# A selective-scan kernel: the input of every fourth state made by ScalarE and TensorE instead of GpSimd

## The chip, the cores and the metric

The kernel runs on one core of one Trainium2 chip (trn2). The core has five engines that work side by side, each through its own instructions in order: TensorE (PE, matrix products and transposes), VectorE (DVE), ScalarE (ACT), GpSimd (POOL) and SyncE (SP, which here only issues the transfers). The metric is the device time in microseconds (us) from launch to end, the median of several runs.

## The reference

Sixteen sequences `x[b]` of 256 steps by 256 features go through four layers that are conditioned on a vector per sequence: a low-rank adapter, a two-way selective state-space layer with an MLP, an attention layer with 16 heads of 64, and an attention layer with 16 heads of 16. Nearly all the time goes into the second one. For each sequence and each of two directions (the backward one runs on the flipped sequence) it computes, with 512 channels d and 64 states s:

```python
xz = h @ in_w;  xs, z = split(xz);  xs = silu(xs)
proj = xs @ xproj_w
dt = softplus(proj[:, :512] + dt_bias);  Bm, Cm = proj[:, 512:576], proj[:, 576:]
A = -exp(A_log)
# for every time t:
hst = hst * exp(dt_t[:, None] * A) + (dt_t * x_t)[:, None] * B_t[None, :]
y_t = einsum('ds,s->d', hst, C_t)
# then
out = ((y + xs * Dskip) * silu(z)) @ out_w
```

For one state s that is: a decay `exp(dt * A[:, s])` for all channels and times, an input `dt * x * B[:, s]`, a scan along time, a multiply by `C[:, s]`, and a sum over the 64 states.

## The kernel before

**Layout.** A channel lies on a partition and time runs along the free dimension, so one state of one sequence and direction is a tile `h` of 128 partitions by 4 channel chunks by 256 times (128x1024 f32). There are 32 units (sequence, direction) and 64 states in each: 2048 steps `k`, taken one after another in the main loop (L1145).

**A step** takes these parts:
- `drive(k + 4)`, L913: four steps ahead. Each four states `load_b` has the DMA spread four rows of B over all partitions (tile `bb`, 512 KB); each eight states `load_c` does so for three rows of C (tile `cb`, 384 KB). Then POOL multiplies `dtx` by a row of `bb` into a fresh `h` (L931). At state 0 ACT also makes `skip = xs * D` (L926).
- `scan(k)`, L965: DVE scans `h` in place in two halves of 512 elements (L974), with the decays as the other operand. For the backward direction it reads `h` from the end. Then `h` is multiplied by C. For states with s % 8 in (0, 2, 3, 5, 6) DVE does it (L977), and C comes from the PSUM tile `cs`; for the other three of each eight POOL does it (L981), from `cb`.
- `decay(k + 1)`, L935: ACT writes the four decays of the next state (L946, one for each chunk, the scale being a column of A) into two of three PSUM banks `decays`, which go round by halves of a state. Column 0 of each chunk holds a zero written once, which starts the scan afresh in each chunk, so a decay covers 255 elements.
- `add_up(k - 2)`, L984: TensorE transposes `h` and adds it to the PSUM tile `y` (eight 128x128 transposes, L992). After that the buffer of `h` is free; there are NH = 11 of them.
- `spread`, L955: TensorE spreads a column of the transposed C (`cT`) into `cs` by two transposes (L961), two such states ahead.

PSUM's eight banks are: three `decays`, one `cs`, two for `y`, two that all other work shares (`bank1`, `bank2`).

**Beside the steps** run generators, of which each step advances two: `pend` (the end of the unit before: `back`, L465, then the projections of the unit after: `front`, L373) and `other` (`rest`, L729: MLP and both attention layers of a finished sequence). `front` makes `xz` (L398, L399), `bc` and its copy in DRAM `bd`, `cT`, `dt` and `dtx` (the last by POOL, L452 to L461). The order in which each engine gets its instructions is a planner's: the order of the program sets priorities, and only calls marked `keep_in_program_order` are held to it. The transfers all go through SP's queue in order. After the last unit, the rest of the last sequence runs alone, and takes the PSUM banks of the scan as well (`alone`, L1183).

Of the kernel before, what the change touches and what calls it, by code (L numbers as in the profile page):

```python
# [23 lines left out]
EPS = 1e-5  # L24

# [29 lines left out]
def kernel(ctx: ExitStack, tc: tile.TileContext, a: dict, out: bass.AP):  # L55
# [69 lines left out]
    ND = 3  # L125
    NH = 11
# [8 lines left out]
    ps_c = ctx.enter_context(tc.tile_pool(name="ps_c", bufs=1, space=PSUM))  # L135
# [120 lines left out]
    for d in ("fwd", "bwd"):  # L256
# [3 lines left out]
        nc.vector.tensor_scalar(an, an, -1.0, None, ALU.mult)  # L260
# [6 lines left out]

    decays = [ps_y.tile([P, 2, T], F32, name=f"decay{j}") for j in range(ND)]
    for dc in decays:
        nc.vector.memset(dc[:, :, 0:1], 0.0)  # L270
# [102 lines left out]
    def front(u):  # L373
# [14 lines left out]
        xz = s2.tile([P, 2 * IC, T], F32, name="xz")  # L388
        for m in range(0, 2 * IC, 2):
            px = halves(bank1("pxz"))  # L390
            for j in range(2):
                for c in range(DC):
                    nc.tensor.matmul(  # L393
                        px[:, j], w_in[:, c, (m + j) * P : (m + j + 1) * P], hT[:, c],
                        start=(c == 0), stop=(c == DC - 1),
                    )
                yield
            nc.scalar.copy(xz[:, m : m + 2], px)  # L398
        nc.scalar.activation(xz, xz, AF.Silu)  # L399
# [3 lines left out]
        for c in range(IC):  # L403
            nc.tensor.matmul(pb[:, :T], w_bc[d][:, c], xz[:, c], start=(c == 0), stop=(c == IC - 1))
# [5 lines left out]
        pt = bank1("pct")  # L410
        for t in range(NT):
            nc.tensor.transpose(pt[:, t * P : (t + 1) * P], bc[:, t * P : (t + 1) * P], ident)
        cT = s2.tile([P, NT, NS], F32, name="cT")
        nc.scalar.copy(cT, pt[:, :T].rearrange("p (t s) -> p t s", t=NT)[:, :, NS:])
        yield


        pr = s1.tile([P, IC, T], F32, name="pr")
        for m in range(0, IC, 2):
            pp = halves(bank1("pdt"))  # L420
            for j in range(2):
                for c in range(IC):
                    nc.tensor.matmul(  # L423
                        pp[:, j], w_dt[:, c, (m + j) * P : (m + j + 1) * P], xz[:, c],
# [36 lines left out]
        tc.keep_in_program_order(nc.gpsimd.tensor_tensor(dtx, dt, xz[:, 0:IC], ALU.mult))  # L461
        st[u] = (xz, cT, bd, dt, dtx)
        yield

    def back(u, yg):  # L465
# [12 lines left out]
        for m in range(DC):  # L478
            xb = xs[b][:, m]
            nc.vector.scalar_tensor_tensor(  # L480
                xb, po[:, m], m_mamba[:, 4 + m, b : b + 1], xb, ALU.mult, ALU.add
# [82 lines left out]
    def heads2(q, k, v, o, rows):  # L564

        exs, exTs = {}, {}
        for i in range(16 + 3):
# [30 lines left out]
            if i % 2 and i >= 3:  # L598
                yield
                po = bank2("po")[:, :T]  # L600
                for h in (i - 3, i - 2):
                    exT = exTs.pop(h)
                    base = (h % 2) * 64
                    for kt in range(NT):
                        nc.tensor.matmul(  # L605
                            po[base : base + 64], v[:, kt, h * 64 : (h + 1) * 64], exT[:, kt],
# [57 lines left out]
    def heads3(q, k, v, oT):  # L664
# [28 lines left out]
        def values(g):  # L693
# [15 lines left out]
            for j in range(4):  # L709
                for kt in range(NT):  # L710
# [182 lines left out]
    bbs, cbs, ys, made, hs, skips = {}, {}, {}, {}, {}, {}  # L893
    cs = ps_c.tile([P, 2, T], F32, name="cs")
    steps = [(u, s) for u in range(len(units)) for s in range(NS)]
    turn = [0]

    def load_b(u, g):
        bd = st[u][2]
        bb = s3.tile([P, SG, T], F32, name="bb")  # L900
        nc.sync.dma_start(bb, bd[g * SG : (g + 1) * SG, :].partition_broadcast(P))
        bbs[u, g] = bb

    def load_c(u, g):
        bd = st[u][2]
        cb = s3.tile([P, 3, T], F32, name="cb")
        nc.sync.dma_start(
            cb,
            bd[NS + 8 * g + 1 : NS + 8 * g + 8 : 3, :].partition_broadcast(P),
        )  # L910
        cbs[u, g] = cb

    def drive(k):  # L913
        u, s = steps[k]
        if s % SG == 0:
# [4 lines left out]
            if s % 8 == 0:  # L920
                load_c(u, s // 8)
        if s == 0:
# [5 lines left out]
        h = s3.tile([P, IC, T], F32, name="h", bufs=NH)  # L928
        bb = bbs[u, s // SG][:, s % SG]
        tc.keep_in_program_order(  # L930
            nc.gpsimd.tensor_tensor(h, st[u][4], bb.unsqueeze(1).to_broadcast([P, IC, T]), ALU.mult)  # L931
        )
        hs[k] = h

    def decay(k):  # L935
        u, s = steps[k]
        d = units[u][1]

        when = slice(1, T) if d == 0 else slice(T - 2, None, -1)
        made[k] = []  # L940
        for i in range(2):
            dc = decays[turn[0] % ND]
            turn[0] += 1
            for j in range(2):
                c = 2 * i + (j if d == 0 else 1 - j)
                nc.scalar.activation(  # L946
                    dc[:, j, 1:T], st[u][3][:, c, when], AF.Exp, scale=a_neg[d][:, c, s : s + 1]
                )
            made[k].append(dc)


    near = [k for k, (u, s) in enumerate(steps) if s % 8 in (0, 2, 3, 5, 6)]
    nth = {k: i for i, k in enumerate(near)}

    def spread(i):  # L955

        if i >= len(near):
            return
        u, s = steps[near[i]]
        for t in range(NT):  # L960
            nc.tensor.transpose(  # L961
                cs[:, i % 2, t * P : (t + 1) * P], st[u][1][:, t, s : s + 1].to_broadcast([P, P]), ident
            )

    def scan(k):  # L965
        u, s = steps[k]
        d = units[u][1]
        h = hs[k]
        for i, dc in enumerate(made.pop(k)):
            hv = h[:, 2 * i : 2 * i + 2].rearrange("p c t -> p (c t)")  # L970
            dv = dc.rearrange("p c t -> p (c t)")
            if d == 1:
                hv = hv[:, ::-1]
            nc.vector.tensor_tensor_scan(hv, dv, hv, 0.0, ALU.mult, ALU.add)  # L974
        if k in nth:
            c = cs[:, nth[k] % 2]
            nc.vector.tensor_tensor(h, h, c.unsqueeze(1).to_broadcast([P, IC, T]), ALU.mult)  # L977
        else:
            c = cbs[u, s // 8][:, (s % 8) // 3]
            tc.keep_in_program_order(  # L980
# [234 lines left out]
```

## Time and profile before

| | |
|---|---|
| median of 3 runs | 7621.71 us (7621.5 to 7629.53) |
| span of the profiled execution | 7616.3 us |
| DVE busy | 6860.6 us (90%) |
| POOL busy | 6843.8 us (90%) |
| PE busy, weight loads | 6249.2 us (82%), 4952.4 us (65%) |
| ACT busy | 5431.2 us (71%) |
| DMA | 675.90 MB, mean 89 GB/s |
| first 400 us / last 226 us: DVE busy | 257.64 / 57.63 us |

The time of the profiled execution itself is not listed apart; its span, from the first instruction to the last, lies 5 us under the median of the runs. A row of the profile's groups reads: line, engine, operation, output<-inputs, shapes, count | busy us, mean ns of one | idle time just before, and who ended it. Instructions of one engine overlap a little, so busy time divided by count is the cost in a sequence, and is a little less than the mean. A matmul's end is modelled, so PE's busy share is not its share of peak.

### The profile page before, as it was taken

How to read it: one execution, taken by the hardware profiler on the slowest of the kernel's cores; microseconds unless marked ns; L12 is line 12 of the kernel's file. 1: busy time of each engine (PE TensorE's matmuls, PEld its weight loads, DVE VectorE, ACT ScalarE, POOL GpSimd, SP SyncE). 2: the span in 40 equal slices, each digit the busy share in tenths (PEclk: the TensorE clock that was granted, in tenths of full speed). 3: DMA queues.
4: the chain of work that ended last, by engine and by line, in shares of the span. 5: the costliest groups of instructions: out<-in, count | busy, mean ns of one | idle time of the engine just before them, and what ended most of it. 6: DMA issues, size and time to landing. Idle time of an engine off the chain costs nothing.

```text
span 7616.3 us, 100847 instructions
## 1 busy us (share of the span) xinstructions
PE 6249.2 (82%) x35471; PEld 4952.4 (65%) x35471; DVE 6860.6 (90%) x6887; ACT 5431.2 (71%) x12141; POOL 6843.8 (90%) x2959
## 2 busy tenths in 40 slices
PE   7568888888888888888888888888888888888778
PEld 4456676666667666676666666666666766666655
DVE  3988999999999999999999999999999999999982
ACT  4567777777777777777777777777777777777753
POOL 3999999999999999999999999999999999999960
PEclk8679999999999999999999999999999999999999
DMA  4112232222322222232222223222232222322221
GB/s 166 54 65 92 89 102 76 87 92 88 103 85 93 80 91 95 92 103 73 88 92 91 100 86 98 78 92 93 87 106 79 94 84 89 101 91 89 73 68 49
DMA packets 331644, 675.90 MB, mean 89 GB/s; under 512 B 24724, under 2 KB 204032, under 8 KB 326784
## 3 DMA queue, kind: packets, MB, share of 16 engines
q1 hardware_dynamic: 331136, 669.44, 26.7%
q8 instruction: 280, 4.59, 0.2%
q14 instruction: 228, 1.87, 0.1%
HBM read 650.22 MB, written 10.75 MB: 87 GB/s over the span
## 4 chain that ended last, share of the span: by engine, by line
DVE 47%; POOL 15%; issue 14%; ACT 12%; PE 10%; DVEq 0%; POOLq 0%; ACTq 0%
DVE h L974 34%; POOL h L931 8%; DVE h L977 8%; ACT decay L946 5%; POOL h L981 5%; PE y L992 3%; DVE maxima L682 1%; ACT L155 1%; PE dense L500 1%; PE down L511 1%; PE bank L108 1%; PE po L605 1%; POOL uu L452 1%; POOL dt L458 1%; POOL dtx L461 1%
## 5 line engine op out<-in xcount | busy, mean ns | idle before, releaser
L974 DVE TENSOR_TENSOR_SCAN h<-decay,h 128x512 f32<-128x512 f32 x4096 | 4748.8, 1213 | 283.1 <-ACT decay L946 196.6
L931 POOL TENSOR_TENSOR h<-dtx,bb 128x1024 f32<-128x1024 f32 x2048 | 4793.5, 2367 | 129.2 <-PE y L992 128.4
L992 PE MATMUL y<-ident,h 128*128 128x128 f32 x16384 | 2385.3, 292 | 693.0 <-POOL h L981 639.1
L992 PEld LDWEIGHTS y<-ident,h 128*128 128x128 f32 x16384 | 2054.6, 151 | 1047.6 <-POOL h L981 733.1
L946 ACT ACTIVATE decay<-dt,a_neg_bwd 128x255 f32<-128x255 f32 x4096 | 1816.8, 471 | 759.9 <-DVE h L974 718.3
L946 ACT ACTIVATE decay<-dt,a_neg_fwd 128x255 f32<-128x255 f32 x4096 | 1824.6, 474 | 613.0 <-DVE h L974 571.6
L981 POOL TENSOR_TENSOR h<-h,cb 128x1024 f32<-128x1024 f32 x768 | 1813.2, 2361 | 289.8 <-DVE h L974 275.1
L977 DVE TENSOR_TENSOR h<-h,cs 128x1024 f32<-128x1024 f32 x1280 | 1533.5, 1215 | 66.2 <-PE cs L961 56.6
L961 PE MATMUL cs<-ident,cT 128*128 128x128 f32 x2560 | 521.6, 294 | 131.8 <-DVE h L977 130.3
L961 PEld LDWEIGHTS cs<-ident,cT 128*128 128x128 f32 x2560 | 331.4, 147 | 216.0 <-DVE h L977 192.0
L572 PE MATMUL sc<-k,q 64*128 64x256 f32 x960 | 293.4, 429 | 16.7 <-ACT ex L581 16.0
L393 PE MATMUL pxz<-hTm,w_in 128*128 128x256 f32 x1024 | 267.6, 388 | 15.9 <-DVE maxima L682 12.1
L679 PE MATMUL sc<-kd,qk 128*128 128x512 f32 x490 | 251.4, 614 | 33.5 <-DVE maxima L682 20.8
L700 PE MATMUL scT<-qk,kd 128*128 128x256 f32 x984 | 251.1, 386 | 28.7 <-DVE qk L691 23.2
L581 ACT ACTIVATE ex<-sc,nmax 128x256 f32<-128x256 f32 x480 | 222.7, 468 | 71.2 <-DVE nmax L577 68.5
L423 PE MATMUL pdt<-xz,w_dt 128*128 128x256 f32 x1024 | 247.3, 385 | 0.0
L572 PEld LDWEIGHTS sc<-k,q 64*128 64x128 f32 x960 | 172.6, 200 | 105.3 <-issue 34.2
L393 PEld LDWEIGHTS pxz<-hTm,w_in 128*128 128x128 f32 x1024 | 181.4, 194 | 53.1 <-DVE maxima L682 15.5
L700 PEld LDWEIGHTS scT<-qk,kd 128*128 128x128 f32 x984 | 175.5, 190 | 60.7 <-ACT pr L429 25.0
L577 DVE TENSOR_REDUCE nmax<-sc 128x2 f32<-128x512 f32 x240 | 163.9, 683 | 49.5 <-PE sc L572 48.8
L423 PEld LDWEIGHTS pdt<-xz,w_dt 128*128 128x128 f32 x1024 | 190.7, 194 | 22.2
L595 ACT COPY exT<-pt 128x512 f32<-128x512 f32 x240 | 140.0, 583 | 86.2 <-PE pt L591 84.0
(350 smaller groups left out, 7571.4 us busy)
## 6 DMA issues: line engine op xcount, KB each, us to landing
bb<-bd SPq DMA_DIRECT2D x512, 512.0 KB
cb<-bd SPq DMA_DIRECT2D x256, 384.0 KB
l2w<-in_L_cond_W_dram SPq DMA_DIRECT2D x32, 1024.0 KB
l3w<-in_L_cond_W_dram SPq DMA_DIRECT2D x32, 1024.0 KB
l1w<-in_L_cond_mlp_w_dram SPq DMA_DIRECT2D x48, 512.0 KB
w_in<-in_L_cond_fwd_in_w_dram SPq DMA_DIRECT2D x16, 1024.0 KB
w_dt<-_L_cond_fwd_xproj_w_dram SPq DMA_DIRECT2D x16, 1024.0 KB
w_in<-in_L_cond_bwd_in_w_dram SPq DMA_DIRECT2D x16, 1024.0 KB
```

The lines of the kernel that those rows point to most:

```text
L393: nc.tensor.matmul(px[:, j], w_in[:, c, (m + j) * P : (m + j + 1) * P], hT[:, c], start=(c == 0), stop=(c == DC - 1),)
L423: nc.tensor.matmul(pp[:, j], w_dt[:, c, (m + j) * P : (m + j + 1) * P], xz[:, c], start=(c == 0), stop=(c == IC - 1),)
L572: nc.tensor.matmul(sc[:, t], q[base : base + 64, ch, t * P : (t + 1) * P], k[base : base + 64, ch], start=True, stop=True,)
L679: nc.tensor.matmul(sc, q[:, g, t * P : (t + 1) * P], kd[g % 2][:, 2 * i : 2 * i + 2], start=True, stop=True)
L700: nc.tensor.matmul(sc[:, kt], kd[g % 2][:, j, kt * P : (kt + 1) * P], q[:, g], start=True, stop=True)
L931: nc.gpsimd.tensor_tensor(h, st[u][4], bb.unsqueeze(1).to_broadcast([P, IC, T]), ALU.mult)
L946: nc.scalar.activation(dc[:, j, 1:T], st[u][3][:, c, when], AF.Exp, scale=a_neg[d][:, c, s : s + 1])
L961: nc.tensor.transpose(cs[:, i % 2, t * P : (t + 1) * P], st[u][1][:, t, s : s + 1].to_broadcast([P, P]), ident)
L974: nc.vector.tensor_tensor_scan(hv, dv, hv, 0.0, ALU.mult, ALU.add)
L977: nc.vector.tensor_tensor(h, h, c.unsqueeze(1).to_broadcast([P, IC, T]), ALU.mult)
L981: nc.gpsimd.tensor_tensor(h, h, c.unsqueeze(1).to_broadcast([P, IC, T]), ALU.mult)
L992: nc.tensor.matmul(ys[u][:, t, c * P : (c + 1) * P], h[:, c, t * P : (t + 1) * P], ident, start=(s == 0 and n == 0 and c == 0), stop=(s == ...
```

## The change

Work moves between engines for every fourth state (s % 4 == 3):
- Its input is no longer made by POOL. Once per unit `turn` has TensorE transpose `dtx` (8 transposes) and ACT copy it to `xT`, time on partitions (2 copies of 128x512). For each fourth state `scale` has ACT multiply `xT` by the column of B (`bT`, per partition) in two activations of 128x512, and `put_in` has TensorE transpose the result (8 transposes) into PSUM. Its decays go to SBUF, into the `h` tile, and the scan takes decays from SBUF and inputs from PSUM.
- The four PSUM banks of the scan (three `decays` and `cs` before) become two `slots` of two banks, one for even and one for odd states, written and scanned by halves. A state's decays, or the fourth state's inputs, go there. The scan of an even state writes its result to its slot in PSUM; that of an odd state to `h`.
- The multiply by C, whole for 1024 elements, is DVE's for even states (from the slot to `h`) and POOL's for odd ones. C comes by DMA for all states: `cb` has four rows each four states (512 KB), `bb` three (384 KB). `spread` and `cs` go.
- For the backward direction `xz` is turned when it is copied from PSUM, and the result of `back` is read turned, so scans and decays run forward. Decays cover 256 elements; `dt` gets 1e34 in column 0 (POOL, once per unit), whose decay is zero, and A is held below -1e-30.
- `xz` becomes `xv` (one buffer) and `zv`, and Silu runs on each. NH falls from 11 to 10. In two attention products beside the scan the matmuls are put in another order (heads inside, key halves outside).

```diff
-        nc.vector.tensor_scalar(an, an, -1.0, None, ALU.mult)
+        nc.vector.tensor_scalar(an, an, -1.0, LEAST, ALU.mult, ALU.min)
...
-    decays = [ps_y.tile([P, 2, T], F32, name=f"decay{j}") for j in range(ND)]
+    slots = [ps_y.tile([P, IC, T], F32, name=f"slot{j}") for j in range(2)]
...
-            nc.scalar.copy(xz[:, m : m + 2], px)
-        nc.scalar.activation(xz, xz, AF.Silu)
+            to = (xv, zv)[m // IC][:, m % IC : m % IC + 2]
+            nc.scalar.copy(to, px[:, :, ::-1] if d else px)
+        for v in (xv, zv):
+            nc.scalar.activation(v, v, AF.Silu)
...
+        tc.keep_in_program_order(nc.gpsimd.memset(dt[:, :, 0:1], APART))
...
-                for h in (i - 3, i - 2):
-                    exT = exTs.pop(h)
-                    base = (h % 2) * 64
-                    for kt in range(NT):
+                for kt in range(NT):
+                    for h in (i - 3, i - 2):
+                        base = (h % 2) * 64
...
-        bb = s3.tile([P, SG, T], F32, name="bb")
+        bb = s3.tile([P, SG - 1, T], F32, name="bb")
...
+    def turn(u):
+        xT = s1.tile([P, NT, DI], F32, name="xT")
+        for t in range(NT):
+            pt = bank1("pxt")
+            for c in range(IC):
+                nc.tensor.transpose(pt[:, c * P : (c + 1) * P], st[u][4][:, c, t * P : (t + 1) * P], ident)
+            nc.scalar.copy(xT[:, t], pt)
+        xTs[u] = xT
...
-        cb = s3.tile([P, 3, T], F32, name="cb")
+        cb = s3.tile([P, SG, T], F32, name="cb")
+        nc.sync.dma_start(cb, bd[NS + g * SG : NS + (g + 1) * SG, :].partition_broadcast(P))
...
-        h = s3.tile([P, IC, T], F32, name="h", bufs=NH)
-        bb = bbs[u, s // SG][:, s % SG]
+        if s % SG < SG - 1:
+            h = s3.tile([P, IC, T], F32, name="h", bufs=NH)
+            bb = bbs[u, s // SG][:, s % SG]
...
+        if s % SG < SG - 1:
+            dcs = two(s)
+        else:
+            h = hs[k] = s3.tile([P, IC, T], F32, name="h", bufs=NH)
+            dcs = h[:, 0:2], h[:, 2:4]
+        for c in range(IC):
+            nc.scalar.activation(
+                dcs[c // 2][:, c % 2], st[u][3][:, c], AF.Exp, scale=a_neg[d][:, c, s : s + 1]
+            )
+
+    def scale(k):
+        u, s = steps[k]
+        sx = s1.tile([P, NT, DI], F32, name="sx")
+        for t in range(NT):
+            nc.scalar.mul(sx[:, t], xTs[u][:, t], st[u][5][:, t, s : s + 1])
+        scaled[k] = sx
+
+    def put_in(k):
+        sx = scaled.pop(k)
+        for c in range(IC):
+            for t in range(NT):
+                nc.tensor.transpose(
+                    two(steps[k][1])[c // 2][:, c % 2, t * P : (t + 1) * P], sx[:, t, c * P : (c + 1) * P], ident
                 )
...
+        c = cbs[u, s // SG][:, s % SG].unsqueeze(1).to_broadcast([P, IC, T])
+        for i, ps in enumerate(two(s)):
+            hv = h[:, 2 * i : 2 * i + 2]
+            d0, d1 = (hv, ps) if s % SG == SG - 1 else (ps, hv)
+            to = hv if s % 2 else ps
+            nc.vector.tensor_tensor_scan(flat(to), flat(d0), flat(d1), 0.0, ALU.mult, ALU.add)
+        if s % 2 == 0:
+            nc.vector.tensor_tensor(h, slots[0], c, ALU.mult)
         else:
+            tc.keep_in_program_order(nc.gpsimd.tensor_tensor(h, h, c, ALU.mult))
...
             scan(k)
             if k + 1 < len(steps):
-                decay(k + 1)
+                if s % SG == SG - 2:
+                    put_in(k + 1)
+                else:
+                    decay(k + 1)
+                if s % SG == SG - 3:
+                    scale(k + 2)
+                    decay(k + 2)
+            if s == NS - 2 and k + 2 < len(steps):
+                turn(u + 1)
```

## The prediction

> **What bounds the kernel now.** I read the busy line of the page first, then the costliest groups, then one steady stretch cut out by time, then the waits inside that stretch.
>
> ```profile
> PE 6249.2 (82%) x35471; PEld 4952.4 (65%) x35471; DVE 6860.6 (90%) x6887; ACT 5431.2 (71%) x12141; POOL 6843.8 (90%) x2959
> ...
> DVE 47%; POOL 15%; issue 14%; ACT 12%; PE 10%; DVEq 0%; POOLq 0%; ACTq 0%
> ```
>
> DVE and POOL are level at 90%, and the chain that ends last runs mostly on DVE. The groups say on what:
>
> ```profile
> L974 DVE TENSOR_TENSOR_SCAN h<-decay,h 128x512 f32<-128x512 f32 x4096 | 4748.8, 1213 | 283.1 <-ACT decay L946 196.6
> L931 POOL TENSOR_TENSOR h<-dtx,bb 128x1024 f32<-128x1024 f32 x2048 | 4793.5, 2367 | 129.2 <-PE y L992 128.4
> ...
> L946 ACT ACTIVATE decay<-dt,a_neg_bwd 128x255 f32<-128x255 f32 x4096 | 1816.8, 471 | 759.9 <-DVE h L974 718.3
> L946 ACT ACTIVATE decay<-dt,a_neg_fwd 128x255 f32<-128x255 f32 x4096 | 1824.6, 474 | 613.0 <-DVE h L974 571.6
> L981 POOL TENSOR_TENSOR h<-h,cb 128x1024 f32<-128x1024 f32 x768 | 1813.2, 2361 | 289.8 <-DVE h L974 275.1
> L977 DVE TENSOR_TENSOR h<-h,cs 128x1024 f32<-128x1024 f32 x1280 | 1533.5, 1215 | 66.2 <-PE cs L961 56.6
> ```
>
> Busy time over count gives what one costs in sequence: a scan 1.159 us, a multiply by C 1.198 on DVE and 2.361 on POOL, an input multiply 2.341 on POOL, a decay 0.4445 on ACT. ACT's long idle time ahead of the decays is ACT waiting for DVE to free a bank: ACT has room.
>
> The steady stretch runs from one unit's four-scan piece in the chain to the same piece 18 units later, so it holds 288 rounds of four states:
>
> ```profile
> 3060.25:7142.51 4082.26, 3423.34 (x19785) 2719.70 (x19784) 3830.89 (x3836) 3038.78 (x6822) 3848.47 (x1657) 0.95 0.28 90
> ```
>
> The columns are length, then PE, PEld, DVE, ACT and POOL busy. Over 288, **a round takes 14.17 us, with DVE busy 13.30, POOL 13.36, PE 11.89, ACT 10.55**. The waits inside that stretch (total, times, longest):
>
> ```profile
> ACT decay L946 <- DVE h L974: 679.6, 781, 4.6
> ...
> DVE h L974 <- ACT decay L946: 113.7, 116, 3.2
> ...
> ACT q L609 <- PE po L605: 82.2, 36, 4.9
> POOL h L931 <- PE y L992: 79.8, 54, 5.8
> ...
> DVE h L974 <- POOL h L931: 41.0, 27, 2.5
> ```
>
> With DVE's smaller waits in the same answer (23.9 for cs; for branch work 25.7 at nmax, 22.9 for the layer norm's bank, 16.4 for a dense product) DVE waits per round 0.395 us for decays, 0.14 for POOL's inputs, 0.08 for cs and 0.23 for branch work: 13.30 + 0.85 + 0.03 unlisted = 14.17. So DVE sets the rate, POOL right beside it.
>
> **The change, per round of four states (512 rounds in the run).**
>
> *DVE.* Multiplies by C fall from 2.5 to 2 a round: 256 fewer x 1.198 = 307 us, or 0.60 a round, so 12.70. The 4096 scans stay. For even states the scan now writes PSUM and the multiply reads PSUM and the cb tile. No row has a scan that writes PSUM. The nearest pair is L804 against L1173, the same 128x512 multiply with its PSUM operand in the one place and the other, at 670 and 689 ns; 19 ns on 2048 scans is 39 us either way (0.08 a round). I take nothing and keep the 0.08 in the range: the scan already reads PSUM, and at 1.16 us for 512 elements it is paced by its recurrence.
>
> *POOL.* It loses 512 input multiplies (x 2.341 = 1198) and gains 256 multiplies by C (x 2.361 = 604): -594 us, 1.16 a round, so 12.20. One small memset a unit is nothing. DVE's wait on POOL (0.14) should shrink; I take half.
>
> *TensorE.* 4096 + 256 transposes come, 2560 (cs) go. At y's price (2385.3 / 16384 = 0.146 us) for the new ones that is 635 - 522 = +113 us, at cs's own price (0.204) +366: 0.2 to 0.7 a round, so at most 12.6. PE stays under DVE. The put_in transposes stand ahead of add_up on PE and need the scan two states back and the scaled input. That scan is over by then, and add_up's y is only needed when a buffer comes round, so I add nothing. DVE's wait for cs (0.08) goes. The two attention products that are reordered (176.0 and 88.8 us busy) may cost anything from all to half of that; PE isn't the bound, so nothing is entered.
>
> *ScalarE.* This pays. The rows:
>
> ```profile
> L399 ACT ACTIVATE xz<-xz 128x2048 f32<-128x2048 f32 x32 | 61.3, 1916 | 0.4
> ...
> L926 ACT ACTIVATE skip<-xz,colb 128x256 f32<-128x256 f32 x128 | 60.1, 496 | 0.0
> ...
> L105 ACT ACTIVATE sq<-hT 128x512 f32<-128x512 f32 x80 | 49.9, 624 | 58.1 <-DVE hT L103 57.8
> ```
>
> L926 is an SBUF activation with a per-partition scale, as the new scaling is, at 60.1 / 128 = 0.470 for 256 elements. L399 against L105 gives (1916 - 624) / 1536 = 0.84 ns an element, so 512 elements cost 0.470 + 0.215 = 0.685. 1024 x 0.685 = 701 us. The 2048 decays that go to SBUF cost L926's 0.470 instead of 0.4445: +52. turn: 64 copies at L1165's 582 ns, +37. Silu in two pieces: 32 x (2 x 1.06, L738's row, - 1.92) = +7. **Together +797 us, 1.56 a round, so ACT is busy 12.11.**
>
> The Trainium skill (ScalarE: Activation LUTs, What ACT_TABLE_LOAD costs) gives 186 ns + 0.833 ns an element, 93 ns more per pointer operand, and back-to-back activations overlapping by 93. That makes 613 ns of the scaling and 73 us less in all; L926's row shows an overlap of 496 - 470 = 26 ns, so the row decides. The same page (Rules for kernel authors) says to multiply on VectorE rather than ScalarE. It speaks against this change, but here VectorE is what sets the rate: 1024 multiplies there at no less than the 485 ns of L550's 128x256 row would add 497 us, about 1 us a round, and eat the gain.
>
> *DMA.* bb shrinks from 512 to 384 KB; cb becomes 512 KB every four states rather than 384 every eight. That is +192 KB a round on DMA engines that are 28% busy. A cb is issued when POOL's last multiply of two groups before is done, about four states (13 us) before its first use; no wait for bb or cb shows in the list of waits. SP issues in order, so weight loads queued behind it move a little. Nothing.
>
> *Buffers.* NH falls from 11 to 10, but the h of every fourth state is taken two states ahead rather than four. POOL's wait for y (79.8 in the stretch) is on an engine that gains 1.16. Nothing.
>
> **The sum.** DVE: 12.70 + 0.23 + 0.03 + 0.07 = 13.03, plus x, its wait for ACT. Today x is 0.395 with ACT's margin at 14.17 - 10.55 = 3.62.
> - If x stays, as decays have their own bank pair per parity and every fourth is made early: 13.42, i.e. -0.75 x 512 = -386.
> - If x grows as ACT's margin shrinks (x times margin constant): x(x + 0.92) = 1.43, x = 0.82, round 13.85, -167.
> I take 0.70, nearer the second, since ACT's margin is what visibly goes: round 13.73, -0.45 x 512 = -230. The profiled execution's span is 7616.3, so 7386; the median of the runs shown, 7621.7, lies 5 above the span, so **7390**.
>
> **Rivals.**
> 1. *ACT's own waits don't shrink.* In the stretch ACT also waits 312 us for PE and DVE outside the decays (1.08 a round; the po row above is the largest). If all of it stands, ACT needs 13.19, its margin was really 2.54, and x(x - 0.16) = 1.00 gives x = 1.09: round 14.11, -32 us, about 7590. For: those waits are in order on ACT. Against: an ACT that arrives later finds PE done, and POOL, which PE's y waits for, gets lighter.
> 2. *Slower: the even bank pair becomes a handshake.* An even state's decays may not start before the multiply by C two states before has read the whole slot; DVE then has two scans (2.32 us) until it needs the first half, which takes 0.9. If ACT comes to it more than 1.4 us late, DVE stands still. ACT now has runs of ten (4 decays, 2 scalings, 4 decays: 5.0 us) in each round, and with them all branch work shifts. Break-even is x = 14.17 - 13.03 = 1.15, 0.57 us at each even state. With 0.8 at both, x = 1.6: round 14.63, +230, about 7850. For: today's longest wait on a decay, 3.2 us, already stands behind table loads on ACT. Against: odd states have more cover than today (a whole scan and a multiply more).
> 3. *The change doesn't do what it says,* because POOL's relief is worth nothing where DVE is as full: then only DVE's 0.60 counts, which is the sum above already; and if its rows grow by the 0.08, the times rise by 40.
>
> **How the numbers follow.** Forecast, x from 0.4 to 0.85, 7230 to 7460: 0.55. Rival 1, x to 1.1, 7460 to 7606: 0.15. Within 0.2% (about what a measurement of this kernel can tell from no change): 0.06. Rival 2: 0.24, the nearer half of it below 7700. Faster 0.70, same 0.06, slower 0.24. The range is 7220 to 7700.
>
> **What would show it.** Right: DVE's C row at 1024 x 1.2 us; POOL busy near 6250; ACT near 6230; DVE still the busiest; its wait for decays 300 to 420 us; no wait for cs or cb. Wrong: scans longer than 1.21 us; the scaling row far from 0.7 us; waits for decays over 590 (rival 2), most of them at even states; a DVE wait on put_in or on a cb transfer; PE above DVE.

## The result and the profile after

| | before | after |
|---|---|---|
| median | 7621.6 us (7614.78 to 7629.53) | 8841.83 us (8838.73 to 8845.57) |
| span of the profiled execution | 7616.3 us | 8843.6 us |
| DVE busy / idle | 6860.6 / 755.7 us | 6771.8 / 2071.8 us |
| mean granted TensorE clock | 0.932 | 0.894 |

The changed kernel is slower: four runs of each give a ratio of 1.160, with a 95% interval of 1.159 to 1.162.

The first line of the page after, each engine's busy time with its share of the span:

```profile
PE 6841.7 (77%) x37263; PEld 5390.0 (61%) x37263; DVE 6771.8 (77%) x6628; ACT 6181.8 (70%) x13323; POOL 6267.4 (71%) x2735
```

The work did move: POOL lost 576 us, DVE 89, ACT gained 751. But no engine is over 77% now, where DVE and POOL stood at 90%. With every engine idle for 23% of the span or more, no single one of them accounts for the span any longer; the engines stand waiting for one another, and the question is for what. The costliest groups after:

```profile
L935 POOL TENSOR_TENSOR h<-dtx,bb 128x1024 f32<-128x1024 f32 x1536 | 3607.8, 2361 | 370.1 <-PE y L996 368.8
L986 POOL TENSOR_TENSOR h<-h,cb 128x1024 f32<-128x1024 f32 x1024 | 2416.7, 2360 | 1823.9 <-DVE h L982 1164.9
...
L982 DVE TENSOR_TENSOR_SCAN slot<-slot,h 128x512 f32<-128x512 f32 x2048 | 2506.0, 1224 | 924.1 <-ACT slot L948 753.5
...
L982 DVE TENSOR_TENSOR_SCAN h<-h,slot 128x512 f32<-128x512 f32 x1024 | 1217.7, 1205 | 274.7 <-PE slot L963 170.7
L982 DVE TENSOR_TENSOR_SCAN h<-slot,h 128x512 f32<-128x512 f32 x1024 | 1207.9, 1206 | 238.6 <-ACT slot L948 225.4
L984 DVE TENSOR_TENSOR h<-slot,cb 128x1024 f32<-128x1024 f32 x1024 | 1241.9, 1213 | 16.9
L956 ACT ACTIVATE sx<-xT,bT 128x512 f32<-128x512 f32 x1024 | 708.3, 713 | 477.7 <-PE slot L963 477.3
```

The scan is now three rows, and each names its state: `slot<-slot,h` is an even state, `h<-slot,h` an odd one, `h<-h,slot` the fourth. Even states wait most, for decays. POOL stands idle for 1824 us before its multiplies by C, where it was 290 before the change. The waits of the whole run, all engines (total, times, longest):

```profile
POOL h L986 <- DVE h L982: 1164.9, 325, 19.6
...
ACT slot L948 <- DVE h L984: 884.5, 663, 5.0
DVE slot L982 <- ACT slot L948: 753.5, 444, 41.1
ACT sx L956 <- PE slot L963: 477.3, 239, 4.1
...
DVE h L982 <- ACT slot L948: 225.4, 174, 4.5
...
DVE nmax L578 <- PE sc L573: 182.9, 93, 4.1
```

The same view of the kernel before has these:

```profile
ACT decay L946 <- DVE h L974: 1289.9, 1443, 6.2
...
DVE h L974 <- ACT decay L946: 196.6, 199, 3.2
...
DVE nmax L577 <- PE sc L572: 48.8, 32, 3.4
```

Read rows two and three of the view after together: DVE waits for ACT's decays, and ACT waits before those decays for DVE's multiply by C. Before, ACT waited for DVE a great deal and DVE for ACT hardly at all, as one expects where DVE sets the rate. Now the waits are long in both directions. That looks like a handshake, two engines that stand still for each other in turn, and not like a load.

With the wait for the fourth state's decays (85.0, from the same view) DVE waits 1064 us for decays, against 196.6 before. The gap of the two spans, 1227.3 us, divides on DVE into: busy -88.8, waits for decays +867, waits for the fourth input +171, waits of an attention maximum for its scores +134 (48.8 before), all else +144.

One such wait, from the timeline after (start, length, engine, line; in brackets the idle time before and who ended it):

```profile
5028.53 1.22 DVE L984 TENSOR_TENSOR h<-slot,cb 128x1024 f32<-128x1024 f32 x1
...
5030.03 2.88 ACT L948 ACTIVATE slot<-dt,a_neg_fwd 128x256 f32<-128x256 f32 x7
...
5032.61 1.22 DVE L982 TENSOR_TENSOR_SCAN h<-slot,h 128x512 f32<-128x512 f32 x1 [2.87 <-ACT slot L948]
5032.84 1.71 ACT L948 ACTIVATE h<-dt,a_neg_fwd 128x256 f32<-128x256 f32 x4
```

DVE ends its multiply at 5029.75 and then waits 2.87 us for an odd state's decays. In the order of ACT's instructions that string of seven, and one decay of the odd state 2.7 us before it, are these (the profile leaves buffer numbers out; they come from the program, whose order of ACT's instructions is that of the trace. `slot1` is the odd state's, `slot0` the next even one's):

```
slot1<-dt,a_neg_fwd   [waits for DVE]       at 5027.32
...
slot0<-dt,a_neg_fwd   [waits for DVE, ACT]  the string from 5030.03
slot1<-dt,a_neg_fwd   [waits for ACT]
slot0<-dt,a_neg_fwd   [waits for ACT]
slot1<-dt,a_neg_fwd   [waits for ACT]
slot0<-dt,a_neg_fwd   [waits for ACT]
slot1<-dt,a_neg_fwd   [waits for ACT]
slot0<-dt,a_neg_fwd   [waits for ACT]
```

The planner lets the two states' decays alternate. The string's first has to wait until DVE's multiply has read all of `slot0`, and the odd decays stand behind it. DVE starts its *first half* at 5032.61, just when the sixth of the seven, the odd state's fourth decay, is written (6 x 0.41 = 2.5 us after 5030.03). The half reads only the first two, of which the second was written after two of the string: four decays, some 1.6 us, were waited for and not read by it. A count over the whole run, of the semaphores that the scans wait for (those that read decays from a slot), says that this is the rule:

```
                       first half waits for ScalarE   second half waits for ScalarE
before, all states            2015 of 2048                   2015 of 2048
after, odd states              497 of 512                    never
after, even states            1024 of 1024                   never
```

The slot is one tile of two banks. A first half waits until all four decays of the tile are written, and then the second half has nothing left to wait for. In the other direction too: the first decay of a state waits for the last reader of the whole tile. Before, each bank was a tile of its own, so both halves waited, each for its own two decays. That gives the theory the runs begin with.

### The profile page after: what moved, and what is told of

It is laid out like the page before. It is cut to its first block, busy times and chain, and to the rows that moved or that the text cites. A ratio compares the mean times of both kernels' runs of the same rounds, so it can differ in the third digit from the quotient of the medians.

```text
span 8843.6 us, 106251 instructions
## 1 busy us (share of the span) xinstructions
PE 6841.7 (77%) x37263; PEld 5390.0 (61%) x37263; DVE 6771.8 (77%) x6628; ACT 6181.8 (70%) x13323; POOL 6267.4 (71%) x2735
## 5 line engine op out<-in xcount | busy, mean ns | idle before, releaser
L935 POOL TENSOR_TENSOR h<-dtx,bb 128x1024 f32<-128x1024 f32 x1536 | 3607.8, 2361 | 370.1 <-PE y L996 368.8
L986 POOL TENSOR_TENSOR h<-h,cb 128x1024 f32<-128x1024 f32 x1024 | 2416.7, 2360 | 1823.9 <-DVE h L982 1164.9
L996 PE MATMUL y<-ident,h 128*128 128x128 f32 x16384 | 2543.1, 313 | 947.9 <-DVE h L984 901.5
L982 DVE TENSOR_TENSOR_SCAN slot<-slot,h 128x512 f32<-128x512 f32 x2048 | 2506.0, 1224 | 924.1 <-ACT slot L948 753.5
L948 ACT ACTIVATE slot<-dt,a_neg_bwd 128x256 f32<-128x256 f32 x3072 | 1389.3, 469 | 770.9 <-DVE h L984 506.0
L948 ACT ACTIVATE slot<-dt,a_neg_fwd 128x256 f32<-128x256 f32 x3072 | 1400.9, 470 | 517.2 <-DVE h L984 378.5
L982 DVE TENSOR_TENSOR_SCAN h<-h,slot 128x512 f32<-128x512 f32 x1024 | 1217.7, 1205 | 274.7 <-PE slot L963 170.7
L982 DVE TENSOR_TENSOR_SCAN h<-slot,h 128x512 f32<-128x512 f32 x1024 | 1207.9, 1206 | 238.6 <-ACT slot L948 225.4
L984 DVE TENSOR_TENSOR h<-slot,cb 128x1024 f32<-128x1024 f32 x1024 | 1241.9, 1213 | 16.9
L956 ACT ACTIVATE sx<-xT,bT 128x512 f32<-128x512 f32 x1024 | 708.3, 713 | 477.7 <-PE slot L963 477.3
L963 PE MATMUL slot<-ident,sx 128*128 128x128 f32 x4096 | 624.5, 297 | 176.6 <-DVE h L982 124.4
```

The lines of the kernel that those rows point to most:

```text
L948: nc.scalar.activation(dcs[c // 2][:, c % 2], st[u][3][:, c], AF.Exp, scale=a_neg[d][:, c, s : s + 1])
L956: nc.scalar.mul(sx[:, t], xTs[u][:, t], st[u][5][:, t, s : s + 1])
L963: nc.tensor.transpose(two(steps[k][1])[c // 2][:, c % 2, t * P : (t + 1) * P], sx[:, t, c * P : (c + 1) * P], ident)
L982: nc.vector.tensor_tensor_scan(flat(to), flat(d0), flat(d1), 0.0, ALU.mult, ALU.add)
L984: nc.vector.tensor_tensor(h, slots[0], c, ALU.mult)
L986: tc.keep_in_program_order(nc.gpsimd.tensor_tensor(h, h, c, ALU.mult))
```

## The experiments

Theory A: the slots, tiles of two banks, are handed over whole. Rivals: B, the work added to ACT (scalings) and its one buffer `sx`; C, the order in which DVE gets its work; D, the fourth state's transposes on TensorE; E, the reordered attention products; F, POOL's half of the multiplies by C. The expectations say theory 1 for A, theories 2 and 4 for B (the buffer, the added work) and theory 3 for C. All times are of one run each unless said; the kernel before ran at 7624 to 7631 us beside them.

**The slots in four tiles of one bank (A).** The multiply by C of even states becomes two of 512 elements.

```diff
-    slots = [ps_y.tile([P, IC, T], F32, name=f"slot{j}") for j in range(2)]
+    slots = [[ps_y.tile([P, 2, T], F32, name=f"slot{j}{i}") for i in range(2)] for j in range(2)]
...
-            nc.vector.tensor_tensor(h, slots[0], c, ALU.mult)
+            for i, ps in enumerate(slots[0]):
+                nc.vector.tensor_tensor(h[:, 2 * i : 2 * i + 2], ps, c[:, 2 * i : 2 * i + 2], ALU.mult)
```

> The changed kernel with the two slots of two banks made four tiles of one bank each, and with it the even multiply by C made in two halves (1024 more DVE instructions, about 100 us of DVE). Theory 1, whole-slot hand-over: in the changed kernel's instructions the first half of a scan waits for all four decays and the first decay for both halves of the scan before, because a slot is one tile; with one tile per bank the time falls to 7700 or less, and DVE's waits for decays in the slots from 979 us to under 400. Theory 2, the single sx buffer holds ACT: no help, 8750 to 8950. Theory 3, the planner's order of instructions doesn't fit the chip: 8400 to 8950, as the order is planned anew but by the same costs. Theory 4, the added ACT work itself: 8750 to 8950.

Measured: 8335.14 us, 507 less, though the C multiplies in halves cost DVE 1343.8 - 1241.9 = 102 us more. The expected 7700 or less was missed by 635 us. DVE's waits in it:

```profile
DVE slot L981 <- POOL h L935: 330.7, 160, 40.3
DVE nmax L578 <- PE sc L573: 232.9, 143, 6.6
DVE slot L981 <- ACT slot L948: 224.7, 148, 4.2
DVE h L981 <- PE slot L963: 214.7, 109, 7.0
DVE h L981 <- ACT slot L948: 91.8, 132, 1.5
```

The waits for slot decays fall from 979 to 316 us, under the 400 that theory 1 named. So A holds, for 507 of 1220 us. One thing came along with the split: the planner gave ACT another order. In the changed kernel 2993 of the 6143 neighbouring pairs of slot decays belong to two different states, and with four tiles 1848. How much of the 507 us is the hand-over itself and how much this order was not separated; ACT's order was held fixed only in the four tiles (below). The rest now stands at POOL's inputs (80.7 before the change, hardly any right after it) and at the fourth state's transposes.

**The scaled input with more buffers (B).** `sx` taken from the ring of `h`, eleven buffers: in the changed kernel, and in the four tiles.

```diff
-    NH = 10
+    NH = 11
...
-        sx = s1.tile([P, NT, DI], F32, name="sx")
+        sx = s3.tile([P, NT, DI], F32, name="sx", tag="h", bufs=NH)
```

> The changed kernel with sx taken from the ring of h buffers (NH 11 in place of 10), so that a scaling doesn't wait for the transposes of the round before. Theory 2: ACT's 477 us of waits at sx go and the time falls by 350 to 480, to 8350 to 8500. Theory 1: under 150 less, since ACT then waits at the slots instead; 8700 to 8850. Theories 3 and 4: as theory 1.

> The four one-bank tiles of the first experiment together with sx from the ring. If the remaining 700 us over the kernel before are theory 2's (sx waits for transposes of the round before), 8000 or less; by theory 1 alone, where what is left is the slot that an even state holds until its multiply by C is over, 8250 to 8400.

Measured: 8831.80 and 8366.36 us: nothing, and 31 more. ACT's wait for the transposes before the scalings (477 us) is gone in the first, and the row ahead of the slot decays has grown from 884.5 to this:

```profile
ACT slot L948 <- DVE h L984: 1123.4, 638, 8.8
```

ACT's other row ahead of these decays, for DVE's scans (L982), has grown from 334.0 to 493.6. ACT now waits at the next instruction instead, so its wait at `sx` was no cause of the loss.

**DVE in program order (C).** Scans and DVE's multiplies by C marked `keep_in_program_order`: in the changed kernel, in the four tiles, and in these with ACT's decays and scalings marked as well.

```diff
-            nc.vector.tensor_tensor_scan(flat(to), flat(d0), flat(d1), 0.0, ALU.mult, ALU.add)
+            tc.keep_in_program_order(nc.vector.tensor_tensor_scan(flat(to), flat(d0), flat(d1), 0.0, ALU.mult, ALU.add))
...
```

> The changed kernel with DVE's scans and multiplies by C held to the order of the program (as POOL's already are), so that the planner can't put halves of two states in turn or put off a multiply by C. Theory 3: under 8300, and the wait of ACT's decays for the multiply by C (884 us) halves. Theories 1, 2 and 4: within 2% of 8842.

> Four one-bank tiles with DVE's scans and multiplies by C held to the order of the program. If the planner's order on DVE (halves of two states in turn, multiplies put off) costs what is left, 7900 or less; otherwise 8250 to 8450, as holding it did nothing to the changed kernel itself.

> Four one-bank tiles, with both DVE's scans and multiplies and ACT's decays and scalings held to the order of the program. If the planner's order on ACT (scalings a round ahead, decays of two states mixed) matters as well, under 7900; otherwise 8250 to 8450.

Measured: 8825.37, 8545.33 and 8698.60 us: nothing, 210 worse and 363 worse. The last two lie outside both ranges of their expectations. Holding DVE to the order of the program recovers nothing, so C has no support; other orders were not tried. Why a fixed order is worse with four tiles was not followed up.

**No fourth-state path at all (D, B).** POOL makes all inputs, all decays go to slots; `turn`, `scale`, `put_in` are gone. Nothing of the result is left out. Once with whole slots, once with four tiles.

```diff
-        if s % SG < SG - 1:
-            dcs = two(s)
-        else:
-            h = hs[k] = s3.tile([P, IC, T], F32, name="h", bufs=NH)
-            dcs = h[:, 0:2], h[:, 2:4]
+        dcs = two(s)
...
```

> The changed kernel without its treatment of the fourth state: no turn, scale or put_in, POOL makes all inputs, all decays go to the slots. POOL then has six multiplies a round, 14.6 us with its other work, so 7900 is a floor. Theories 2 and 4 (the fourth state's work on ACT is the cause): 7900 to 8100. Theory 1: the slots still change hands whole, 8300 to 9000. Theory 3: anything, 7900 to 8900.

> Four one-bank tiles, and no treatment of the fourth state (POOL makes all inputs; floor 7900 by POOL's six multiplies a round). If the hand-over of whole slots was all that held it, 7900 to 8000. If two slots with the even one held through the multiply by C are short by themselves, 8200 or more. If the fourth state's chain over ACT, PE, DVE and POOL is what the first experiment still loses, under 8000.

Measured: 8598.03 and 8092.51 us, 506 apart: the whole slots cost the same with the fourth-state path (507) and without it. The page of the second:

```profile
PE 6258.8 (77%) x32911; PEld 4876.8 (60%) x32911; DVE 6687.1 (83%) x7652; ACT 5443.2 (67%) x12235; POOL 7419.9 (92%) x3247
```

POOL is the busiest here at 92%, with 1024 multiplies by C beside all 2048 inputs, so this pair prices the slots and not D. 8092 lies between the ranges of its expectation.

**The parts of the fourth state's input, by leaving them out (D against B).** From the four tiles, first without `put_in` (scalings and `turn` stay), then without `scale` and `turn` as well. In both the fourth state's scan reads what the slot last held, so its input is missing from the computation.

```diff
                 if s % SG == SG - 2:
-                    put_in(k + 1)
+                    scaled.pop(k + 1)
```

> As the run before, but with turn and the scalings kept on ACT, and only put_in left out; the fourth state's input is missing from the result here too. If ACT's load costs, this stands near 8335 and well above the run before; if the chain through PE into the slot costs, it stands within 100 us of the run before.

> Four one-bank tiles, and the fourth state's input left out: no turn, no scaling on ACT, no transposes by put_in; its scan takes what the state before left in the slot, so that part of the computation is missing. It shows what the fourth state's input costs at most, POOL staying at five multiplies a round. If the input's path (ACT's 700 us, or the chain over ACT and PE) is what the four tiles still lose against the kernel before (8335 against 7627), 7300 to 7600. If the slots themselves or the order of the instructions lose it, 8000 or more.

Measured: 7679.91 and 7585.96 us. From 8335, **`put_in` is worth 655 us and then all of ACT's new scaling, with `turn`, 94.** They were left out in this order only. The page of the last one:

```profile
PE 6078.6 (80%) x32911; PEld 4775.1 (63%) x32911; DVE 6645.5 (88%) x7652; ACT 5436.9 (72%) x12235; POOL 6257.4 (83%) x2735
```

DVE sets the rate again. And 7586 is only 45 us, 0.6%, under the kernel before: even with the fourth state's input for nothing, four tiles gain almost nothing. `put_in`'s transposes are some 4096 x 0.15 = 620 us on TensorE, which is not the busiest engine in either kernel (80% in both). That they cost 655 us of *time* suggests that it matters where they stand and not only how long they are; a run below moves them without making them shorter.

**The even state's scan back to `h` (is it the scan that writes PSUM?).** From the four tiles; C is then one DVE multiply of two SBUF tiles.

```diff
-            to = hv if s % 2 else ps
+            to = hv
...
+            nc.vector.tensor_tensor(h, h, c, ALU.mult)
```

> Four one-bank tiles, and the scan of an even state writes h in SBUF, so that its bank is free after the scan; DVE then multiplies h by cb whole, with both inputs in SBUF (100 us of DVE back). Theory 1 with the held slot: 7500 to 7900, ACT's 700 us of waits for the multiply by C gone. Rival, DVE and POOL getting into each other's way when DVE reads two SBUF inputs: POOL's 2.36 us rises to 2.7 or more, or DVE's 1.21 us to 1.5 or more, and the time stays over 8200.

Measured: 9335.68 us, 1000 *worse*. Two groups of this kernel:

```profile
L935 POOL TENSOR_TENSOR h<-dtx,bb 128x1024 f32<-128x1024 f32 x1536 | 4138.9, 2708 | 0.0
...
L983 DVE TENSOR_TENSOR h<-h,cb 128x1024 f32<-128x1024 f32 x1024 | 2193.5, 2142 | 25.1
```

The same multiply takes 2142 ns with both inputs in SBUF and 1213 with one in PSUM, and POOL's input multiply goes from 2361 to 2708. That is the rival which the expectation names, on all three of its signs, so the run doesn't tell what the held slot costs; it shows what it costs to take both operands of this multiply from SBUF. The last section reads it.

**The attention products alone (E).** The kernel before, with only their matmuls reordered (8 runs against 9).

```diff
-                for h in (i - 3, i - 2):
-                    exT = exTs.pop(h)
-                    base = (h % 2) * 64
-                    for kt in range(NT):
+                for kt in range(NT):
+                    for h in (i - 3, i - 2):
+                        base = (h % 2) * 64
```

> The kernel before with only the two attention products put in the new order (heads inside, key halves outside). The prediction entered nothing; at most half of 265 us of TensorE goes. Expected 7560 to 7640. If the order of matmuls with 64 or 32 columns mattered for the change's loss, it would be slower than 7640.

Measured: 7618.53 against 7626.24 us, ratio 0.999, interval 0.998 to 1.000. No effect that can be told from none, in the kernel before; in the changed kernel the order was not tried by itself.

**Other states for POOL (F).** From the four tiles: POOL multiplies states 1 and 2 of each four by C, DVE 0 and 3, so that POOL never waits for the fourth's scan.

```diff
-            to = hv if s % 2 else ps
+            to = ps if s % SG in (0, 3) else hv
...
-        if s % 2 == 0:
-            for i, ps in enumerate(slots[0]):
+        if s % SG in (0, 3):
+            for i, ps in enumerate(two(s)):
```

> Four one-bank tiles; POOL multiplies states 1 and 2 of each four by C and DVE states 0 and 3 (the fourth from its slot, into which its scan then writes), in place of POOL 1 and 3. If what put_in costs (655 us) comes from POOL standing in line behind the fourth state, whose input has the longest way, 7700 to 8000. If it comes from the way through PE into the slot itself, 8250 or more; it may be worse, since the fourth state then holds its slot through the multiply as well.

Measured: 8445.71 us, 111 worse, the second branch of the expectation. DVE waits 289 us for `put_in` in it, against 215 in the four tiles. But the fourth state also holds its slot longer here, so the run alone doesn't rule F out.

**POOL's multiply one step later (F).** From the four tiles: it is issued after the next step's input multiply, and `add_up` runs three steps behind rather than two.

```diff
+            late_c[k + 1] = h, c
...
-    AHEAD, BEHIND = 4, 2
+    AHEAD, BEHIND = 4, 3
...
                 drive(k + AHEAD)
+            multiply(k)
             scan(k)
```

> Four one-bank tiles; POOL's multiply by C of a state is put one step later in POOL's order, behind one more input multiply, and the sum on PE a step later too. If POOL's place in line matters, 300 us or more go (8050 or less); if not, 8250 to 8450.

Measured: 8135.02 us, 200 less, between the two ranges of the expectation. DVE's 331 us of waits for POOL's inputs are 78.5 here.

**`put_in` one state earlier (D).** From the four tiles: the scaling and the transposes come right after the scan that frees their slot (state 1), ahead of decays, rather than after the next one (state 2).

```diff
-                if s % SG == SG - 2:
-                    put_in(k + 1)
-                else:
-                    decay(k + 1)
                 if s % SG == SG - 3:
                     scale(k + 2)
+                    put_in(k + 2)
+                if s % SG != SG - 2:
+                    decay(k + 1)
+                if s % SG == SG - 3:
                     decay(k + 2)
```

> Four one-bank tiles; the scaling and put_in are given to the planner one state earlier, right behind the scan that frees the slot and ahead of the sums and the branch work of that step. If the inputs of the fourth state come late because put_in stands behind other work on PE, 300 us or more go (8050 or less). If the wait is for the slot itself, within 100 us of 8335.

Measured: 7916.71 us, 418 less, with the same work. Its page and DVE's waits:

```profile
PE 6432.2 (81%) x37263; PEld 5133.6 (65%) x37263; DVE 6689.6 (85%) x7652; ACT 6084.9 (77%) x13319; POOL 6255.5 (79%) x2735
```

```profile
DVE slot L981 <- POOL h L935: 221.0, 88, 40.5
DVE nmax L578 <- PE sc L573: 137.2, 90, 4.8
DVE slot L981 <- ACT slot L948: 113.5, 111, 2.5
DVE x L530 <- PE down L512: 103.3, 29, 6.1
DVE h L981 <- PE slot L963: 92.5, 37, 5.0
```

Against the four tiles, the wait for `put_in` (214.7) has shrunk by 122, that for POOL's inputs by 110, that of even states for slot decays by 111 and that of the attention maximum by 96; some rows of the work beside the steps have grown, the `x` row above most. The move touches only the first of these directly, so the others fit engines that stood in line behind it. Of the 655 us that `put_in` is worth, 418 thus come back by an earlier place for it and its scaling; whether the other 237 are still its place, or its length, is not shown.

**Both, then the scaling earlier still.** The last two edits together; then with `scale` at state 0 as well.

```diff
                 if s % SG == SG - 3:
-                    scale(k + 2)
                     put_in(k + 2)
...
+                if s % SG == 0:
+                    scale(k + 3)
```

> Four one-bank tiles with both changes of place: put_in one state earlier (418 us alone) and POOL's multiply by C one step later (200 us alone). If they mend different waits, 7700 to 7800; if they mend the same one, 7850 to 7950.

> As the run before, and the scalings a state earlier still, so that the scaled input lies ready when the scan frees the slot. If ACT's burst of two scalings ahead of put_in is part of the way, 50 to 150 us less than the run before; if sx with its single buffer then holds ACT, the same or more. Below 7600 it would beat the kernel before.

Measured: 7876.27 and 7825.57 us. Moving POOL's multiply gave 200 alone and 40 after `put_in` had been moved: the two edits mend the same loss for 160 of the 200. That fits one chain, in which the fourth state's scan waits for `put_in`, POOL's multiply by C for that scan, and POOL's next inputs stand behind the multiply in its queue. The earlier scaling gave another 51. 7826 is the best that keeps all of the computation, 1016 under the changed kernel and still 202 us (2.7%) above the kernel before beside it. So no version here beats the kernel before.

**The early `put_in` with whole slots.** The changed kernel with the edit of `put_in` alone.

> The changed kernel as it is, slots of two banks in one tile, with only the scaling and put_in given to the planner one state earlier. If the two causes (whole slots, and put_in's place on PE) are independent, 418 us less than 8842: 8350 to 8500. If with whole slots the place doesn't matter, because the slot is free later anyway, 8700 or more.

Measured: 8815.61 us, 26 less, where the same edit gave 418 with four tiles. While slots are handed over whole, DVE's largest wait keeps its size (753.5 in the changed kernel):

```profile
DVE slot L982 <- ACT slot L948: 772.6, 422, 41.5
```

The two gains don't add up; that of the early `put_in` shows only when the whole slots are gone.

## Why the prediction was wrong

Its busy times were mostly right and its waits were not, and the forecast was a sum of both.

- **POOL** at 6250: 6267.4. **ACT** at 6230: 6181.8. **The scaling** at 0.685 us: 708.3 / 1024 = 0.692. **DVE's multiply by C** at 1.2: 1241.9 / 1024 = 1.213. "No wait for cs or cb" was right also: DVE's multiply by C waits 16.9 us in all. The overlap of 26 ns that the prediction read from L926's row is a misreading: a row's busy time takes off only the overlap among its own instructions. In the trace before, the instruction after an L926 starts 94 ns before its end, on average over the 97 of 128 that overlap, close to the 93 that the prediction set aside. It cost the sum little: ACT gained 751 us, not 797.
- **The scans** were entered at the old price, with 0.08 a round (39 us) as the bound of writing PSUM. DVE's busy time came to 6771.8 rather than 6860.6 - 307 = 6554. The even states' scans cost 2506.0 / 2048 = 1.224 us, 0.065 above the 1.159 before, which is 132 us; the others are 1.18 to 1.19. About half of it goes with the shared tile, for in the four tiles the even scan is 1.194. Most of the rest seems to go with writing PSUM: in the run with the result in `h`, even and odd scans together are 1.166. The rows of these two runs:

```profile
L981 DVE TENSOR_TENSOR_SCAN slot<-slot,h 128x512 f32<-128x512 f32 x2048 | 2445.7, 1217 | 598.0 <-POOL h L935 330.7
...
L981 DVE TENSOR_TENSOR_SCAN h<-slot,h 128x512 f32<-128x512 f32 x3072 | 3580.5, 1204 | 840.0 <-POOL h L935 611.1
```

  What the shared tile does is seen in the timeline after, at an even pair and an odd pair of halves:

```profile
4405.96 2.50 DVE L982 TENSOR_TENSOR_SCAN slot<-slot,h 128x512 f32<-128x512 f32 x2
...
4409.64 2.33 DVE L982 TENSOR_TENSOR_SCAN h<-slot,h 128x512 f32<-128x512 f32 x2
```

  Even halves don't overlap: by the count of semaphores above, each of the 1024 second halves waits for DVE itself, since both halves write one tile.
- **The wait for decays, x, failed, and with it the forecast.** The prediction took 0.70 us a round from ACT's margin; measured are 1064 / 512 = 2.08. The step that failed is in rival 2, and the forecast leant on the same picture: "until it needs the first half, which takes 0.9". The diff showed `slots` as one tile of four chunks where `decays` were tiles of two, and the prediction read "written and scanned by halves" without asking by what unit the *waits* are set. They are set by the tile. The first half needs all four decays (1.6 us at 0.40 each) and ACT may begin only when both halves are free. Splitting the tiles gives 507 and 506 us back in the two pairings, ACT's new order included. Rival 2 had the direction, the handshake, and the place (753.5 of the waits are at even states), but put x at 1.6. The forecast's span was 7386 and 8843.6 came, a miss of about 1457 us. By the rows, some 710 of it are x, 218 DVE's busy time, 171 the wait for the fourth input, 134 the attention maximum's wait for its scores, and the rest other waits.
- **"so I add nothing" for `put_in` was the second failed step.** The scan two states back is indeed over by then, but in its place the transposes stand where DVE's fourth scan needs them at once, and POOL and TensorE's later work behind that. It is 655 us in the four tiles, of which one state's earlier place recovers 418. Its wait row alone (215 us in the four tiles) shows a third of it.
- **TensorE** was put at 6363 to 6615 and came to 6841.7. `put_in` cost 624.5 / 4096 = 0.152, near y's price as taken; but y itself rose from 2385.3 to 2543.1, in a run whose clock is lower, 0.894 against 0.932. PE came to stand above DVE (6771.8), one of the signs of being wrong that the prediction had set; scans over 1.21 us, waits for decays over 590, most of them at even states, and a wait on `put_in` are the others that came.
- **ACT's load**, on which forecast and rival 1 turned ("This pays"), is worth 94 us of time in the four tiles without `put_in`. The reordering of the attention products was rightly entered at nothing, as far as the kernel before shows it.
- **The gain that was expected of DVE and POOL** did not come even with the fourth input left out and the tiles split: 7586 against 7631. DVE is 215 us less busy there, but stands idle for 183 more, and its waits for POOL's inputs are 152 us, against 81 before, though POOL is 586 us less busy. What this kernel would do without the waits of its slots was not run.

Left open: what makes up the last 200 us of the best version over the kernel before (its DVE waits are 177 for the attention scores, 198 for slot decays, 105 for `hd` and 56 for transfers of `cb`, none of them dominant), what of the 507 us is the order that the planner gives ACT, and why a fixed order on DVE costs 210 us with four tiles.

## What to carry to other kernels

Read a buffer's tile, and not only the slices an instruction names, to see what a wait is for: two banks in one tile are one hand-over, and here splitting them was worth 507 us although it took 1024 more instructions. When a change takes an engine's input from two other engines instead of one, price the place of the new work in their queues as well as its duration, and try it one step earlier. If all engines are at 70 to 77% after a change that was to relieve the busiest, look for pairs of waits that name each other and have grown long in both directions, and expect that a second cause shows only when the first is taken away.

## What the hardware showed that was not expected

**A DVE multiply with both inputs in SBUF excludes POOL.** The prediction did not have this; the expectation of the run with the result in `h` names it as a rival. In that kernel the multiply took 1194 ns at its shortest, 2208 at the median and 3436 at its longest. The timeline of one:

```profile
5019.87 2.35 POOL L985 TENSOR_TENSOR h<-h,cb 128x1024 f32<-128x1024 f32 x1 [0.20 <-POOL h L935]
5020.89 2.41 DVE L983 TENSOR_TENSOR h<-h,cb 128x1024 f32<-128x1024 f32 x1
...
5022.17 3.32 POOL L935 TENSOR_TENSOR h<-dtx,bb 128x1024 f32<-128x1024 f32 x1
```

DVE starts at 5020.89 while POOL runs until 5022.22, and ends at 5023.30: 1.08 after POOL, about the time it needs alone. POOL's next multiply starts at 5022.17 and takes 3.32 rather than 2.36, about 1 us longer: it waits for DVE in turn. The Trainium skill says so (SBUF — State Buffer, Who interferes with whom): DVE's second pair of SBUF ports is GpSimd's, and it is held as an exclusive lock. The rows agree: 1213 ns with an operand in PSUM, 2142 without.

**The granted clock was lower, by and large, where TensorE stood more.** It was 0.932 before, with TensorE busy for 82% of the span, 0.894 after (77%), 0.905 in the four tiles (80%) and 0.938 with the early `put_in` (81%), while y's 16384 transposes went from 2385.3 us before to 2543.1 after. It doesn't go with the time: without the fourth input, at 7586 us, it was 0.908 (80%). These are five kernels and no test of the cause; but in the changed kernel the waits came together with slower matmuls.
